# A graph layer on one core: features, destinations and penalties loaded two chunks at a time in three buffers, where four chunks at a time in two buffers were loaded before

## The chip, the core and the metric

The kernel runs on one core of one Trainium2 chip. The core has five instruction streams that wait for each other only through semaphores: PE (matrix multiply; loads of its stationary operand are shown apart as PEld), DVE (vector), ACT (scalar functions), POOL (GpSimd) and SP (SyncE, which here only issues transfers). ACT and SP issue plain transfers, GpSimd the indirect ones. The metric is the device time of one execution in microseconds; the median of the runs counts.

## The reference, cut to what matters

```python
h = maximum(layernorm(x), 0)                      # x: 12500 nodes x 32
e_feat = concatenate([h[src], h[dst], edge_attr]) # 400000 edges, sorted by dst
v = relu(e_feat @ W1 + b1) @ W2 + b2              # 96 -> 64 -> 32
x_cand = segment_max(v, dst, num_segments=12500)
return x + maximum(x_cand, h)
```

## The kernel before, in words

The edges are cut into four stripes of 100000, and a stripe into 196 chunks of C = 512 edges. One chunk of all four stripes is handled at once: partition = stripe x 32 features, 512 edges along the free axis. The first layer is a sum of three parts, each a product with a slice of W1, added up in four PSUM tiles `ph`: the edge's own features `ea` (L506), the destination's part, and the source's part `ht` (L548).

The **source** features come in two ways. For each chunk, 12 of 16 groups of 128 edges are fetched by GpSimd: one indirect transfer each (L154), from the normalised node table `h_d` in device memory into tiles `gh`, three to a tile, 24 tiles in turn; DVE then transposes each tile (L256). The other 4 groups are made by PE with one-hot matrices (`tile`, L238): 14 matmuls for each group of 128 edges, against the node features held on chip; DVE and ACT make the one-hots (L207, L216, L217), and DVE picks the right node of each result (L242, L243). Source indices of all chunks are on chip from the start.

The **destination** part uses that edges are sorted: a chunk's destinations lie in a window of 32 nodes. A window of precomputed products is fetched from `q_d` to `qw` (L456, four small transfers a chunk, their addresses read into SP's registers), and a one-hot `of` of destination against window row is made by ACT from `db`, the chunk's destinations repeated over 32 partitions (L462, L463).

After the second layer (L569), DVE's scan (L576) takes the running maximum along the edges; `pb`, a penalty of -1e30 at each first edge of a node, restarts it. Transposes and small matmuls (L476, L486) pick the last edge of each node, ACT copies them to `wo` (L490), and SP writes them to `top_d` (L494, four a chunk). Every write to one of the two `top_d` tables waits for the one before it there.

**Passes.** The loop of L530 handles two chunks in a pass, 98 passes in all. Its code is in a hand-written order, which is kept on SP, PE, DVE and ACT; GpSimd's stream is the gathers, in order. A pass for chunks c, c+1 does, in this order: GpSimd's gathers for c+2, c+3 (L533); the keys `kb` for the one-hots (ACT's queue, L192); `load` for chunks c+4, c+5 (L536); sometimes a block of destination data (`load_block`, L539, ACT's queue); then the matmuls, DVE and ACT work, among which `hid` (L552, needs `ph` complete), `window_hots` for the next pair (L554), `edges_into` and `windows_into` for the next pair (L564, L570), and `leave_1`, `leave_2`, which end the present one.

**`load`** (L437 to L457) is what the change touches. Where the chunk number divides by LOAD it issues three transfers: `ea` on SP, `db` and `pb` on ACT's queue (for the first chunks, before the loop, all on SP: L514). They serve LOAD chunks. With LOAD = 4 that is 1024 KB of `ea`, 1024 KB of `db`, 512 KB of `pb` in every second pass, into two buffers each. For each chunk it also issues the four `qw` transfers on SP, behind the `ea`. `load` runs AHEAD = 4 chunks before the chunk is used. SP's own order in a pass is thus: `ea`, eight `qw`, four `top_d` for chunk c-1, four for chunk c.

**Semaphores.** The framework gives all plain transfers of SP and ACT eight completion semaphores in turn, in one order for both queues, and GpSimd's gathers another eight. A transfer may be issued only when the earlier one that used its semaphore has landed; a queue waits for that, and what is behind waits too.

**Start and end.** Before the loop the nodes are normalised, `h_d` and `q_d` written, and the one-hot tiles of the first two chunks made. After it the two `top_d` tables are read back, their maximum is taken, and the output written (L620 to L703).

Of the kernel before, what the change touches and what calls it, by code (L numbers as in the profile page):

```python
# [8 lines left out]
F32 = mybir.dt.float32  # L9
F32R = mybir.dt.float32r  # L10
F16 = mybir.dt.float16
BF16 = mybir.dt.bfloat16
I32 = mybir.dt.int32
# [10 lines left out]
P = 128  # L24
# [8 lines left out]
C = 512  # L33
# [4 lines left out]
SE = E // NS  # L38
TS = S // P
EP = NS * S  # L40
LOAD = 4
A1 = 7
A0 = NT // A1
MM = 4
# [4 lines left out]
NB = NCH // BLOCK  # L49
# [11 lines left out]
def ap(t, offset, dims):  # L61
    return bass.AP(tensor=t.tensor, offset=t.offset + offset, ap=dims)
# [3 lines left out]
def gnn_kernel(ctx, tc, x, src, src_mm, src_t, dst, dst_ext, lo, lo_c, ends_b, edge_attr, weights, w1, w2, b2, out):  # L66
# [81 lines left out]
    def gather(c):  # L148
        n = min(K - MM * (c in MMC), (SE - c * C) // D)
        parts = []  # L150
        for k in range(0, n, SOME):
            parts.append(gathered.tile([P, SOME, D], F32, name="gh"))
            for i in range(min(SOME, n - k)):
                nc.gpsimd.indirect_dma_start(  # L154
                    out=parts[-1][:, i, :], out_offset=None, in_=h_d[:, :],
                    in_offset=bass.IndirectOffsetOnAxis(ap=src_i[:, c, k + i:k + i + 1], axis=0))
        return parts
# [14 lines left out]
    loaded_b, ats = {}, {}  # L172
# [14 lines left out]
    def load_keys(c, queue=nc.scalar):  # L187

        if c in MMC:
            n = min(2, MMC.stop - c)  # L190
            kb = early.tile([P, 2, MM * P], F16, name="kb", bufs=2)
            queue.dma_start(kb[:, :n], ap(key_d, (c - MMC.start) * MM * P,  # L192
                                           [[0, P], [MM * P, n], [1, MM * P]]))
            for k in range(n):
                keys[c + k] = kb[:, k]
# [31 lines left out]
    def tile(c, m):  # L227

        if c not in MMC:
            return  # L230
        if m == 0:
            mm_rows[c] = early.tile([P, MM, D], F32, name="gm", bufs=6)
        hot = hots[c]
        e = slice(m * P, (m + 1) * P)
        po = early_ps.tile([P, C], F32, name="pv", bufs=2)[:, :D * A0]
        for k in range(A1):
            for part in range(2):
                nc.tensor.matmul(po, hot[:, k, e], hs[:, part, k].rearrange("p f a -> p (f a)"),  # L238
                                 start=(k == 0 and part == 0), stop=(k == A1 - 1 and part == 1))
        of_group = po.rearrange("p (f a) -> p f a", a=A0)  # L240
        one = early.tile([P, D, A0], F32, name="one", bufs=2)
        nc.vector.tensor_tensor(one, of_group, masks[c][:, m, None, :].to_broadcast([P, D, A0]), op=ALU.mult)  # L242
        nc.vector.tensor_reduce(mm_rows[c][:, m, :], one, axis=AX.X, op=ALU.max)  # L243
# [21 lines left out]
    def load_block(b, queue=nc.scalar):  # L265
        edges = early.tile([P, 2, NS * BLOCK, J], I32, name="di")
        queue.dma_start(edges, dst[:, b])
        ends = early.tile([P, 2, NS * BLOCK], I32, name="ends")
        queue.dma_start(ends, ap(ends_b, b * 2 * NS * BLOCK, [[0, P], [NS * BLOCK, 2], [1, NS * BLOCK]]))
        loaded_b[b] = edges[:, 0], edges[:, 1], ends[:, 0], ends[:, 1]  # L270
# [160 lines left out]
    with tc.tile_pool(name="edges", bufs=3) as pool, tc.tile_pool(name="edges_ps", bufs=1, space=PSUM) as ps:  # L431
# [5 lines left out]
        def load(c, queue=nc.scalar):  # L437
            if c % LOAD == 0:
                n = min(LOAD, NCH - c) * C
                ea = pool.tile([P, LOAD * C], F32, name="ea", bufs=2)  # L440
                nc.sync.dma_start(ea[:, :n], ea_v[:, c * C:c * C + n])
                db = pool.tile([P, LOAD * C], I32, name="db", bufs=2)
                pb = pool.tile([P, LOAD * C], BF16, name="pb", bufs=2)
                queue.dma_start(db[:, :n], ap(dst_ext, 1 + c * C, [[S, NS], [0, D], [1, n]]))
                queue.dma_start(pb[:, :n], ap(pen_d, c * C, [[S, NS], [0, D], [1, n]]))
                for k in range(c, min(c + LOAD, NCH)):
                    loaded[k] = [t[:, (k - c) * C:(k - c + 1) * C] for t in (ea, db, pb)]
            if c % 2 == 0:
                _, base = nc.values_load_multi_w_load_instructions(
                    lo_i[0:1, c:c + 2], engines=[SP], min_val=0, max_val=N,  # L450
                    skip_runtime_bounds_check_because="dst is a node, or N where the host pads")
                for k in range(2):
                    bases[c + k] = base[k * NS:(k + 1) * NS]
            qw = pool.tile([P, HID], F32, name="qw", bufs=8)
            for s in range(NS):
                nc.sync.dma_start(qw[s * W:(s + 1) * W, :], q_d[bass.ds(bases[c][s], W), :])  # L456
            windows[c] = qw, bases.pop(c)  # L457

        def window_hots(c):

            of = ofs[c] = pool.tile([P, C], F32, name="of", bufs=3)
            nc.scalar.activation(of, loaded[c][1], AF.Square, bias=below[:, c:c + 1])  # L462
            nc.scalar.activation(of, of, AF.Relu, bias=ones, scale=-1.0)  # L463
# [66 lines left out]
        for c in range(0, NCH, 2):  # L530
            a, b = c + 2, c + 3
            for k in range(a, min(a + 2, NCH)):
                gh[k] = gather(k)  # L533
            load_keys(a + 2)
            for k in range(c + AHEAD, min(c + AHEAD + 2, NCH)):
                load(k)  # L536
            b_next = (c + 3 * AHEAD) // BLOCK
            if c % LOAD and b_next < NB and b_next not in ats and b_next not in loaded_b:
                load_block(b_next)  # L539

            if a == NCH - 2:
                nc.gpsimd.tensor_tensor(again.rearrange("p (g a) f -> p g a f", a=A0),
                                        hs[:, 0].rearrange("p g f a -> p g a f"),
                                        hs[:, 1].rearrange("p g f a -> p g a f"), op=ALU.add)
            tile(a, 0)
            to_features(a, 0)
            ht = [hts.pop(c + x).rearrange("p k e -> p (k e)") for x in range(2)]
            into_ph(ph, [(w1a, ht[x]) for x in range(2)], False, True)  # L548
            hid = []
            for s in range(NS):  # L550
                hid.append(pool.tile([P, C], F32, name="hid", bufs=6))
                nc.scalar.activation(hid[s], ph[s], AF.Relu, bias=b1c)  # L552
            for k in range(a, min(a + 2, NCH)):
                window_hots(k)  # L554
            one_hots_act(b)
            one_hots(b, 0, 2)
            tile(a, 1)
            to_features(a, 1)
            one_hots(b, 2, BY_ACT.start)
            mask_of(b)  # L560
            tile(a, 2)
            to_features(a, 2)
            last = [lasts(c)]
            ph = edges_into(a)  # L564
            pv = [early_ps.tile([P, C], F32, name="pv", bufs=2) for x in range(2)]
            for s in range(NS):
                for x in range(2):
                    g = slice(x * HID, (x + 1) * HID)
                    nc.tensor.matmul(pv[x][s * D:(s + 1) * D], w2x[g], hid[s][g], start=True, stop=True)  # L569
            windows_into(a, ph)  # L570
            leave()
            sms = []
            for x in range(2):
                before = -LOW if sm is None else sm[:, C - 1:C]
                sm = pool.tile([P, C], F32, name="sm", bufs=3)
                nc.vector.tensor_tensor_scan(sm, loaded.pop(c + x)[2], pv[x], before, op0=ALU.add, op1=ALU.max)  # L576
                sms.append(sm)
            tile(a, 3)
            one_hots_act(a + 2)
            to_features(a, 3)  # L580
            to_features(a, J)
            so = leave_1(c, sms[0])
            last.append(lasts(c + 1))
            tile(b, 0)
            to_features(b, 0)
            one_hots(a + 2, 0, 2)
            leave_2(c, so, last[0])
            tile(b, 1)
            to_features(b, 1)
            so = leave_1(c + 1, sms[1])  # L590
            one_hots(a + 2, 2, BY_ACT.start)
            mask_of(a + 2)
            tile(b, 2)
            to_features(b, 2)
            if c == 2 * AHEAD:
                places(FIRST, len(MMC))
            if (c + 4) % BLOCK == 0 and (c + 4) // BLOCK < NB:
                make_block((c + 4) // BLOCK)
            tile(b, 3)
            to_features(b, 3)  # L600
            to_features(b, J)
            leave = lambda c=c + 1, so=so, last=last[1]: leave_2(c, so, last)
# [164 lines left out]
```

## Time and profile before

| what | value |
|---|---|
| time, median of 3 runs | 4203.63 us (4203.39 to 4204.59) |
| the profiled execution's own time | 3066.27 us |
| its span, first to last instruction | 3064.5 us |
| mean granted clock of PE in it | 0.988 |
| PE busy | 2969.0 us, 97% of the span |
| GpSimd busy | 2261.8 us, 74% |
| DVE busy | 2246.8 us, 73% |
| ACT busy | 1089.8 us, 36% |
| transfers | 229.58 MB, 75 GB/s over the span |

The profiled execution is 1137 us shorter than the median of the runs. Durations below are of the profiled one.

The profile gives, for each engine, its busy time, and for groups of like instructions their number, busy time, mean duration in ns and the idle time of the engine just before them, with what ended most of it. "issue" there is time in which the engine waited for nothing that the profile shows. The waits name who waited for whom, with the total in us, how often, and the longest; the release is inferred from semaphores, so where a name had long been done, it was something else. All times within the run count from the start of the span. Since a plain matmul's end is modelled, a busy PE is not PE at its peak.

### The profile page before, as it was taken

Reading aid. Unit: us, or ns where it says so; the run is one execution under the profiler, and the core shown is the slowest. Engines: PE = TensorE matmul, PEld = TensorE weight load, DVE = VectorE, ACT = ScalarE, POOL = GpSimd, SP = SyncE. Lnnn points to the kernel's source line nnn. Section 1 sums busy time; section 2 is a strip of 40 time slices with the busy share of each in tenths; the row PEclk is TensorE's granted clock in tenths of the full one; section 3 lists DMA queues with packets and bytes.
Section 4 is the critical chain, followed back from the end, with each engine's and each line's share of the span. In section 5 each row is a group of like instructions: output and inputs, shape, how many; then the busy total and the mean of one; then the engine's idle time right before and its main releaser. Section 6 shows DMA issues by size and latency. Waiting matters only on the chain. (4 is left out here: it accounts for less than half of the span.)

```text
span 3064.5 us, 58825 instructions
## 1 busy us (share of the span) xinstructions
PE 2969.0 (97%) x21189; PEld 2326.1 (76%) x21189; DVE 2246.8 (73%) x3869; ACT 1089.8 (36%) x1795; POOL 2261.8 (74%) x2376
## 2 busy tenths in 40 slices
PE   5999999999999999999999999999999999999995
PEld 4678787787878777777777777777777777787773
DVE  6577777777777776777777777777777777777775
ACT  4333433333343333333333333333333333333331
POOL 6777777777777777777777777777777777777774
PEclk9899999999999999999999999999999999999997
DMA  7333333234324323332333233333332333333322
GB/s 245 70 85 66 62 79 82 60 66 84 71 59 88 74 59 66 81 76 59 65 82 73 59 69 80 70 63 65 86 70 59 73 82 65 63 70 81 66 57 70
DMA packets 194678, 229.58 MB, mean 75 GB/s; under 512 B 118333, under 2 KB 158797, under 8 KB 181582
## 3 DMA queue, kind: packets, MB, share of 16 engines
q10 hardware_dynamic: 32580, 110.55, 12.6%
q1 hardware_dynamic: 86762, 76.67, 10.8%
q0 software_dynamic: 75040, 38.57, 10.1%
q8 instruction: 167, 2.74, 0.4%
q14 instruction: 129, 1.06, 0.1%
HBM read 211.68 MB, written 13.85 MB: 74 GB/s over the span
## 5 line engine op out<-in xcount | busy, mean ns | idle before, releaser
L154 POOL DMA_INDIRECT gh<-h_d,src_i x2345 | 2241.7, 956 | 758.1 <-issue 537.4
L238 PE MATMUL pv<-hs,hot 128*128 128x448 f32 x10920 | 2359.8, 371 | 13.0 <-DVE sm L576 12.8
L238 PEld LDWEIGHTS pv<-hs,hot 128*128 128x128 f32 x10920 | 2016.0, 188 | 276.0 <-issue 71.0
L242 DVE TENSOR_TENSOR one<-pv,mask 128x448 f32<-128x448 f32 x780 | 483.5, 620 | 676.1 <-PE pv L238 674.6
L552 ACT ACTIVATE hid<-ph,wt 128x512 f32<-128x512 f32 x392 | 237.6, 689 | 1255.7 <-PE ph L500 1164.5
L207 DVE TENSOR_TENSOR hot<-kb,consts 128x1536 fp32r<-128x1536 f16 (+2 forms) x388 | 565.8, 1458 | 0.1
L243 DVE TENSOR_REDUCE gm<-one 128x32 f32<-128x448 f32 x780 | 483.7, 620 | 26.9
L217 ACT ACTIVATE hot<-away,ones 128x512 fp32r<-128x512 f32 x392 | 283.7, 724 | 251.4 <-issue 241.8
L216 ACT ACTIVATE away<-kb,key_n 128x512 f32<-128x512 f16 x392 | 278.0, 709 | 0.0
L256 DVE STREAM_TRANSPOSE ht<-gh 128x96 f32<-128x96 f32 x782 | 210.4, 269 | 68.8 <-DMA gh<-h_d,src_i 67.4
L576 DVE TENSOR_TENSOR_SCAN sm<-pb,sm,pv 128x512 f32<-128x512 bf16 x195 | 247.6, 1270 | 16.2 <-PE pv L569 5.9
L486 PEld LDWEIGHTS tr<-so,last 128*64 128x64 f32 x3136 | 108.4, 138 | 114.2 <-issue 78.7
L490 ACT ACTIVATE wo<-tr 128x64 f32<-128x64 f32 x196 | 44.0, 224 | 391.3 <-PE tr L486 374.0
L462 ACT ACTIVATE of<-db,below 128x512 f32<-128x512 int32 x196 | 141.7, 723 | 19.1 <-DMA db<-in_dst_ext 19.1
L569 PE MATMUL pv<-hid,wt 64*32 64x512 f32 x1568 | 135.1, 606 | 10.0 <-DVE one L242 8.9
L463 ACT ACTIVATE of<-of,ones 128x512 f32<-128x512 f32 x196 | 142.1, 725 | 6.4
L486 PE MATMUL tr<-so,last 128*64 128x64 f32 x3136 | 135.7, 229 | 3.7 <-DVE so L478 3.7
L500 PE MATMUL ph<-of,qw 32*64 32x512 f32 x1568 | 116.6, 623 | 15.6 <-DMA qw<-q_d 15.6
L468 DVE TENSOR_TENSOR last<-consts,at 128x512 f32<-128x512 f32 x196 | 129.9, 663 | 0.0
L478 DVE TENSOR_TENSOR so<-tr,wt 128x512 f32<-128x512 f32 x196 | 127.8, 652 | 2.3 <-PE tr L476 2.3
L476 PE MATMUL tr<-ident,sm 128*128 128x128 f32 x784 | 118.1, 273 | 1.1 <-ACT wo L490 1.1
L500 PE MATMUL ph<-ht,wt 32*64 32x512 f32 x1568 | 114.0, 617 | 0.0
(77 smaller groups left out, 554.4 us busy)
## 6 DMA issues: line engine op xcount, KB each, us to landing
ea<-in_edge_attr SPq DMA_DIRECT2D x49, 1024.0 KB
db<-in_dst_ext ACTq DMA_DIRECT2D x48, 1024.0 KB
gh<-h_d,src_i POOLq DMA_INDIRECT x2345
pb<-pen_d ACTq DMA_DIRECT2D x48, 512.0 KB
kb<-key_d ACTq DMA_DIRECT2D x95, 256.0 KB
qw<-q_d SPq DMA_DIRECT2D x784, 8.0 KB
top_d<-wo SPq DMA_DIRECT2D x784, 4.0 KB
top_d<-zero ACTq DMA_DIRECT2D x2, 1568.0 KB
```

Of the source, the lines that this page charges most:

```text
L154: nc.gpsimd.indirect_dma_start(out=parts[-1][:, i, :], out_offset=None, in_=h_d[:, :], in_offset=bass.IndirectOffsetOnAxis(ap=src_i[:, c, ...
L207: nc.vector.tensor_tensor(hot_of(c)[:, start:stop], keys[c][:, None, :].to_broadcast([P, n, MM * P]), key_ps[:, start:stop, None].to_broad ...
L216: nc.scalar.activation(away, keys[c], AF.Square, bias=key_n[:, k:k + 1])
L217: nc.scalar.activation(hot_of(c)[:, k], away, AF.Relu, bias=ones, scale=-1.0)
L238: nc.tensor.matmul(po, hot[:, k, e], hs[:, part, k].rearrange("p f a -> p (f a)"), start=(k == 0 and part == 0), stop=(k == A1 - 1 and par ...
L242: nc.vector.tensor_tensor(one, of_group, masks[c][:, m, None, :].to_broadcast([P, D, A0]), op=ALU.mult)
L243: nc.vector.tensor_reduce(mm_rows[c][:, m, :], one, axis=AX.X, op=ALU.max)
L256: nc.vector.transpose(ht[:, r].rearrange("p k e -> p (k e)"), gh[c][part][:, :r.stop - r.start].rearrange("p k f -> p (k f)"))
L486: nc.tensor.matmul(pw[g * 2 * W:(g + 1) * 2 * W], last[:, j, 2 * g:2 * g + 2].rearrange("p s w -> p (s w)"), so[:, j, g * 2 * D:(g + 1) * ...
L500: nc.tensor.matmul(ph[s][x * HID:(x + 1) * HID], w[g], e[g], start=start, stop=stop)
L552: nc.scalar.activation(hid[s], ph[s], AF.Relu, bias=b1c)
L576: nc.vector.tensor_tensor_scan(sm, loaded.pop(c + x)[2], pv[x], before, op0=ALU.add, op1=ALU.max)
```

## The change

LOAD becomes 2. The three tiles of `load` lose their own `bufs=2` and take the pool's three buffers. The condition for `load_block` named LOAD and now names the number 4, so blocks are loaded in the same passes as before. Each set of transfers is half as large, and a set is issued in every pass. The buffers of the three tiles shrink from 2 x 20 KB to 3 x 10 KB in each partition. PE's, DVE's and GpSimd's instructions, and their order, are the same in both built programs.

```diff
-LOAD = 4
+LOAD = 2
...
         def load(c, queue=nc.scalar):
             if c % LOAD == 0:
                 n = min(LOAD, NCH - c) * C
-                ea = pool.tile([P, LOAD * C], F32, name="ea", bufs=2)
+                ea = pool.tile([P, LOAD * C], F32, name="ea")
                 nc.sync.dma_start(ea[:, :n], ea_v[:, c * C:c * C + n])
-                db = pool.tile([P, LOAD * C], I32, name="db", bufs=2)
-                pb = pool.tile([P, LOAD * C], BF16, name="pb", bufs=2)
+                db = pool.tile([P, LOAD * C], I32, name="db")
+                pb = pool.tile([P, LOAD * C], BF16, name="pb")
                 queue.dma_start(db[:, :n], ap(dst_ext, 1 + c * C, [[S, NS], [0, D], [1, n]]))
                 queue.dma_start(pb[:, :n], ap(pen_d, c * C, [[S, NS], [0, D], [1, n]]))
...
             b_next = (c + 3 * AHEAD) // BLOCK
-            if c % LOAD and b_next < NB and b_next not in ats and b_next not in loaded_b:
+            if c % 4 and b_next < NB and b_next not in ats and b_next not in loaded_b:
                 load_block(b_next)
```

## What was predicted

> **What bounds the kernel now.** I read the page's engine rows first, then its costliest groups, then GpSimd's timeline in one loop pass, then the stretches of three passes, then the waits (engines, then the queue of SyncE).
>
> ```profile
> PE 2969.0 (97%) x21189; PEld 2326.1 (76%) x21189; DVE 2246.8 (73%) x3869; ACT 1089.8 (36%) x1795; POOL 2261.8 (74%) x2376
> L154 POOL DMA_INDIRECT gh<-h_d,src_i x2345 | 2241.7, 956 | 758.1 <-issue 537.4
> ```
>
> PE at 97% looks like the bound, but GpSimd's 74% misleads: its idle time is mostly the pause after each gather. Three rows of its timeline:
>
> ```profile
> 1543.97 0.96 POOL L154 DMA_INDIRECT gh<-h_d,src_i  x1 [0.30 <-DMA gh<-h_d,src_i]
> 1545.23 0.95 POOL L154 DMA_INDIRECT gh<-h_d,src_i  x1 [0.30 <-issue]
> 1547.20 0.95 POOL L154 DMA_INDIRECT gh<-h_d,src_i  x1 [1.01 <-DVE gm L243]
> ```
>
> One gather starts every 1.26 us at best (0.95 and 0.30). A pass needs 24, so 30.24 us of GpSimd; a pass in which PE never waits lasts 29.73 us (the stretch 1507.42 to 1537.15, one start of the L500 `ht` matmuls to the next). So GpSimd is slower by 0.5 us a pass and lives on its lead: gathers start at 27.7, the loop's first `ht` matmuls at 88.9. By about 1190 the lead is used up, and from there every second pass is longer:
>
> ```profile
> 1507.42:1537.15 29.73, 29.73 (x217) 23.56 (x216) 24.11 (x45) 10.90 (x18) 22.72 (x24) 1.00 0.29 50
> 1537.15:1568.50 31.35, 30.92 (x217) 23.78 (x216) 22.44 (x39) 10.89 (x18) 23.14 (x25) 1.00 0.39 87
> ```
>
> (stretch, its length, busy PE, PEld, DVE, ACT, POOL, granted clock, DMA share, GB/s.) The long pass is the one after a load was issued (L444 at 1525.6, L441 at 1534.5). Its waits are small and one-directional: a gather is late, DVE's transpose L256 waits for it, PE's L569 waits for DVE:
>
> ```profile
> DVE ht L256 <- DMA gh<-h_d,src_i: 61.6, 73, 2.4
> PEld pv L569 <- DVE one L242: 53.5, 60, 2.3
> ```
>
> (waits from 1190 to 3014.) PE's passes from there exceed 29.73 by about 50 us in all. The end, then, follows GpSimd's stream: last gather at 3014.0, then 50.5 us of tail. The stream has 758.1 us of idle; 12.6 is the wait for the first `h_d`, 2344 pauses of 0.305 are 714.9, and 30.6 us remain as real stalls. Sorting those by time since the last L444 issue gives the place: all but 1 us of them lie 12 to 28 us after it, 63 gathers with a pause over 0.4 us, at 48 loads.
>
> Why there: the gathers have eight completion semaphores in turn, so a gather may not start before the one eight earlier has landed, 8 x 1.26 = 10.1 us later. From the trace's semaphore records I took each gather's time to its last increment: 2.4 us (median) 34 to 58 us after a load, but 8.5 to 9.7 us in the first 14 us after it, with a ninth decile of 10.2 to 10.4. The burst puts gathers just over that limit. From 24 to 26 us, when `pb` with its 4096-byte packets is what is left, it is 5.0.
>
> **The change, part by part.** [...]`ea`, `db`, `pb` become 98 transfers each instead of 49, half as large, one set each pass.
>
> Issues. 48 more `db` and 48 more `pb` on ACT cost 0.56 and 0.51 us: 51 us, behind ACT's wait for PE ahead of L552 (1164.5 us in 91 passes, 12.8 each); without that cover `hid` would be 51 us late. 49 more `ea` on SyncE cost 0.42: 21 us, hidden since SyncE sits 15 us late in load passes today and PE does not notice. On GpSimd nothing.
>
> Waits. SyncE's `qw` transfers share eight semaphores with ACT's loads, and today the queue stands behind them:
>
> ```profile
> SPq L456 <- DMA db<-in_dst_ext: 612.6, 49, 14.4
> SPq L456 <- DMA pb<-pen_d: 180.3, 48, 5.3
> ```
>
> That is 16 us a load. The built program keeps such waits, now in every pass: the fourth `qw` on `db`, the sixth on `pb`, the eighth on `ea`. ACT issues `db` about 9 us ahead of SyncE's `ea`, and half of 14.4 is 7.2, so `db` lands before SyncE asks; I take 0 to 4 us for `pb` and `ea`. Behind them stand the `qw` rest and eight `top_d` writes; both have most of a pass to spare, so 0. ACT's `db`, `pb` wait for semaphores last used by the previous `qw` and by the first four `top_d`, all issued by then: 0 to 1 us, under the 12.8. [...]A third buffer frees before it is asked for: its last reader, the scan, ended six us before the next issue (1519.4 against 1525.6).
>
> Gathers, the main term. Half-size transfers have packets of 4096 bytes (`pb` 2048) where 8192 took 586 and 402 ns (queues q1, q10) and 4096 took 159. The nearest row for a 4096-byte burst is the 5.0 us above; add 1 to 2 us for `ea` beside it: 6 to 7 us, well under 10.1. So stalls go from 30.6 to about 0 (value taken: 0.6 left). The bounds: all 30.6 gone, or none, and below nothing the second rival.
>
> The Trainium skill speaks against this: "DMA: Bandwidth & Descriptors", section "Bandwidth", says to batch transfers to 1 MiB or more, with a fixed cost near 2 us each. By it 147 more transfers cost 294 us of transfer time, some of it exposed. By the rows, `db` of 1 MB takes 14 us, 75 GB/s, so size isn't its limit, and the queues fill 33.5% of the engines (12.6, 10.8, 10.1); the fixed cost lies under a pass. I take the rows. The same page, "Queues, rings and completion order", says each engine alternates between the queues by whole packets. By it a gather's packet waits for one packet of each other queue, 586 + 402 ns, so 2.4 becomes 3.4 us, the limit of 10.1 is never met, and the change gains 0 (4203). The rows say 8.7, so more than one packet stands ahead; I keep the rows, and take only that a smaller packet shortens the wait.
>
> Start. PE stands for the first loads: ACT waits 19.1 us for the first `db`, PE 10.5 and 2.5 us for `qw` (77.7, 81.5; SyncE held by `db`, then `pb`), and the granted clock is 0.5 from 72 to 89 us. Half a `db` lands about 10 us earlier, at 62; `pb` at 66; the last needed `qw` at 69. So `windows_into` ends at about 70 instead of 83.4, 13 us, and some of the half clock goes too. But chunks 2 and 3 now come in a second set, whose `qw` wait for `db` and `pb` of two sets together: PE may wait 5 us at 84, where today it waits 4.3. Net 8 to 18 us for PE, and in this profile worth 0: GpSimd started at 27.7 regardless, and PE merely meets it sooner.
>
> Sum on the profiled execution: 3066.3 (span 3064.5, 1.8 around it) - 30 = 3036. PE alone would allow about 3064.5 - 50 - 13 = 3001, so GpSimd is next late, at 30.2 a pass. The medians need a caution: the runs shown take 4203.6, 1137 us above the profiled one, and nothing in the trace says which resource is slower there. Carried over as an absolute amount, 4203.6 - 30 = 4174; in proportion it would be -41, 4162.
>
> **The rivals.**
> - *The gather stalls go, the stream sets the end (likeliest, 0.48):* 4174, down to 4155 if the slower runs have longer bursts.
> - *Only the start counts (0.22):* if PE is what is slower in the runs shown (a pass of about 41 us), gathers are never late and no stall is exposed. For it: PE's clock is the one resource that varies in the trace (1.0, halves at start and end). Gain 4 to 15 us: 4192, about half of it beyond 0.2%.
> - *Nothing moves (0.14):* if gathers are slower there, 1.7 us each, then eight of them last 14 us, over the 9.7 of the burst, and there is no stall to remove: 4203. That the stated halving has no effect on the end is this case too.
> - *Slower (0.16):* bursts come in 97 passes instead of 48, and `ea`, issued 9 us after `db`, joins the gathers' wait. If latency in a burst stays above 10.1 us, each costs what one costs now, 30.6 / 48 = 0.64 us: 97 x 0.64 = 62, so +31: 4235. It decides if halved packets leave more than 10.1 us; against it is the 5.0 row.
>
> **How the numbers follow.** About 0.2% (8 us) is what a measurement of this kernel can tell from no change. Faster: 0.48 + half of 0.22 + a little = 0.61; same: the other half and most of 0.14, 0.23; slower 0.16. Range 4150 to 4212: from the proportional gain with 12 us more to just past no change; it leaves out most of the slower case and a larger gain, under 0.2.
>
> **What would show it.** GpSimd's L154 row: idle 758 falls to about 730, few pauses over 0.4 us; gather landing in a burst 6 to 7 us; passes alternate no more, all about 30.2; last gather near 2984. SyncE's wait on `db` falls from 612 to under 100. First `ht` matmuls near 75. Wrong if pauses stay or come in every pass, if the wait of ACT ahead of L552 vanishes, or if the profile gains its 30 us and the median does not: then what is slower in the unprofiled runs hides the stream.

## The result, and the profile after

The changed kernel took 4283.69 us (median of 5 runs, 4272.22 to 4292.48), the kernel before beside it 4204.29 us (4203.39 to 4208.16): a ratio of 1.0185, 95% interval 1.0171 to 1.0199. It is slower by 79 us, where 30 us of gain were predicted.

One thing has to be said first, since no number below can be read without it: **both kernels have two conditions, the same for all timed runs of one set, and the kernel before takes about 3060 us in one and about 4200 us in the other.** It is not the chip: one chip took 4199 us for the kernel before in one set and 3066 us in a later one. The times above and the profile after are of the second; the profiled execution of the kernel before, from which every duration of the prediction came, was of the first (3066.27 us). I call them the 3060 and the 4200 condition after the time of the kernel before. In the 3060 condition the changed kernel is **faster**: 3026.48 us (4 runs) against 3063.16, ratio 0.9875 (0.9849 to 0.9902).

The profile after is an execution of 4277.61 us, span 4275.5. From its page, the engines, the granted clock in 40 slices, the gathers, and the one-hot matmuls with the idle time before them:

```profile
PE 3533.0 (83%) x21189; PEld 2435.1 (57%) x21189; DVE 2238.1 (52%) x3869; ACT 1111.9 (26%) x1795; POOL 2263.7 (53%) x2376
PEclk7789899999898989899898889898989998988898
L154 POOL DMA_INDIRECT gh<-h_d,src_i x2345 | 2243.1, 957 | 1893.5 <-DVE ht L256 703.5
L238 PE MATMUL pv<-hs,hot 128*128 128x448 f32 x10920 | 2614.8, 385 | 605.1 <-issue 417.6
```

The number of instructions is that of before, and a gather takes 957 ns, as before (956). But GpSimd now waits 1893.5 us, the largest part of it (703.5) for DVE instead of in its own pauses: it is early, not late. DVE's transposes, which need the gathered rows, no longer wait for them; here is their row, first of the kernel before at 3060 (e1_before_again, below), then of the profile after:

```profile
L256 DVE STREAM_TRANSPOSE ht<-gh 128x96 f32<-128x96 f32 x782 | 210.5, 269 | 67.4 <-DMA gh<-h_d,src_i 67.0
L256 DVE STREAM_TRANSPOSE ht<-gh 128x96 f32<-128x96 f32 x782 | 209.8, 268 | 0.0
```

And PE has idle time, 605.1 us ahead of the one-hot matmuls alone, most of it put down to "issue": PE waits for nothing that the profile shows.

The stretches of one pass in the middle and of two near the end (stretch, its length, busy PE, PEld, DVE, ACT, POOL with the number of instructions, granted clock, DMA share, GB/s):

```profile
1869.38:1912.86 43.48, 36.03 (x217) 25.48 (x217) 22.78 (x42) 11.10 (x18) 22.92 (x25) 0.88 0.22 49
4155.25:4184.99 29.74, 29.74 (x217) 23.57 (x216) 22.19 (x38) 10.90 (x18) 11.95 (x1) 1.00 0.20 55
4184.99:4214.72 29.73, 29.73 (x217) 23.56 (x216) 22.19 (x38) 10.89 (x18) 0.00 (x0) 1.00 0.03 7
```

The 216 matmuls of a pass (the view counts one more, cut by the edge) take 43.48 us in the middle and 29.73 at the end. So the condition isn't a slower PE for the whole run. It goes with the gathers, whose last one starts at 4150.8, and not with the loads: the pass from 4155.25 still has a whole set of them (`db` issued at 4173.4, `ea` at 4179.3; 55 GB/s). Inside the slow pass, PE's weight loads show what it is (start, length, group with its count, idle time before and what ended it):

```profile
1870.42 4.18 PEld L238 LDWEIGHTS pv<-hs,hot 128*128 128x128 f32 x21 [0.81 <-issue]
1875.78 0.30 PEld L238 LDWEIGHTS pv<-hs,hot 128*128 128x128 f32 x2 [1.17 <-issue]
1877.92 0.28 PEld L238 LDWEIGHTS pv<-hs,hot 128*128 128x128 f32 x1 [1.84 <-issue]
1878.63 0.29 PEld L238 LDWEIGHTS pv<-hs,hot 128*128 128x128 f32 x1 [0.43 <-issue]
1880.03 0.28 PEld L238 LDWEIGHTS pv<-hs,hot 128*128 128x128 f32 x1 [1.11 <-issue]
```

Up to 1874.4 a weight load starts every 0.20 us. Then they come at distances of 0.7 us and its multiples (1877.92, 1878.63, 1880.03), until about 20 us into the pass. SyncE's register instructions do the same: 293 of them take over 0.3 us, nearly all about 0.7, where none does in the 3060 condition. DVE, ACT and GpSimd keep their durations. I call this the **slow stretch**; every pass of the 4200 condition has one, in the kernel before too. The weight loads shown wait for no semaphore, so their idle time stands as "issue"; waits whose release the profile can't name stand as "remote". The granted clock follows it: 0.84 in the 3 us from 1875.38, then 0.50 in the 3 us from 1878.38. (That a PE with little to do loses half its clock is what the Trainium skill says too, "TensorE: Matmul & The Clock Gate", Part 1; here the half clock lasts about 8 us in each pass, 974 us in all, against 58 in the 3060 condition.)

### The profile page after: what moved, and what is told of

Same layout as the page of the kernel before. It is cut to its first block, busy times and chain, and to the rows that moved or that the text cites. A ratio compares the mean times of both kernels' runs of the same rounds, so it can differ in the third digit from the quotient of the medians.

```text
span 4275.5 us, 59032 instructions
## 1 busy us (share of the span) xinstructions
PE 3533.0 (83%) x21189; PEld 2435.1 (57%) x21189; DVE 2238.1 (52%) x3869; ACT 1111.9 (26%) x1795; POOL 2263.7 (53%) x2376
## 2 busy tenths in 40 slices
DMA packets 214672, 229.60 MB, mean 54 GB/s; under 512 B 119510, under 2 KB 159974, under 8 KB 214119
## 5 line engine op out<-in xcount | busy, mean ns | idle before, releaser
L154 POOL DMA_INDIRECT gh<-h_d,src_i x2345 | 2243.1, 957 | 1893.5 <-DVE ht L256 703.5
L238 PE MATMUL pv<-hs,hot 128*128 128x448 f32 x10920 | 2614.8, 385 | 605.1 <-issue 417.6
L238 PEld LDWEIGHTS pv<-hs,hot 128*128 128x128 f32 x10920 | 2058.2, 194 | 1061.6 <-issue 622.0
L552 ACT ACTIVATE hid<-ph,wt 128x512 f32<-128x512 f32 x392 | 260.6, 687 | 2211.7 <-remote 1016.9
L569 PE MATMUL pv<-hid,wt 64*32 64x512 f32 x1568 | 251.3, 903 | 8.7 <-DVE one L242 7.9
L486 PEld LDWEIGHTS tr<-so,last 128*64 128x64 f32 x3136 | 124.6, 146 | 199.4 <-issue 169.0
L500 PE MATMUL ph<-ea,wt 32*64 32x512 f32 x1568 | 225.4, 1016 | 13.2 <-issue 13.0
L486 PE MATMUL tr<-so,last 128*64 128x64 f32 x3136 | 162.7, 239 | 51.9 <-issue 47.8
L569 PEld LDWEIGHTS pv<-hid,wt 64*32 64x32 f32 x1568 | 37.2, 128 | 230.2 <-issue 118.8
L500 PE MATMUL ph<-of,qw 32*64 32x512 f32 x1568 | 150.4, 825 | 0.1
L500 PE MATMUL ph<-ht,wt 32*64 32x512 f32 x1568 | 127.1, 622 | 7.8 <-issue 5.1
```

The source lines that it names most:

```text
L154: nc.gpsimd.indirect_dma_start(out=parts[-1][:, i, :], out_offset=None, in_=h_d[:, :], in_offset=bass.IndirectOffsetOnAxis(ap=src_i[:, c, ...
L486: nc.tensor.matmul(pw[g * 2 * W:(g + 1) * 2 * W], last[:, j, 2 * g:2 * g + 2].rearrange("p s w -> p (s w)"), so[:, j, g * 2 * D:(g + 1) * ...
L500: nc.tensor.matmul(ph[s][x * HID:(x + 1) * HID], w[g], e[g], start=start, stop=stop)
```

## The experiments

All of them are compared with the kernel before, run beside them. The first set, the third and the last two fell in the 3060 condition, the second in the 4200 condition; a set's condition can't be chosen.

**What the stalls are worth at 3060.** First the kernel before again (e1_before_again), 3062.83 us.

> The kernel before, unchanged, to see its trace at its usual time of 4204 us (the profile shown before was of a run of 3066 us). In the changed kernel's trace nearly every pass has one slow stretch of about 8 us in which SyncE's and PE's instructions take 0.7 us each, and the granted clock drops after it; the last two passes, which load nothing, have none and last 29.7 us. Theory S, a stretch comes with each set of loads: here passes alternate, about 30 us without a load and 53 us with one. Theory T, a stretch comes in every pass whatever is loaded: all passes about 41 us. Theory G, the one of the prediction (late gathers in the bursts): passes of 41 us in which GpSimd never waits for DVE.

It repeats the profile of the prediction: 31.4 us of gather pauses beyond 0.305, 63 of them over 0.4 us, first `ht` matmuls at 85.3, clock 0.988, and two passes of

```profile
1323.12:1352.98 29.86, 29.86 (x218) 23.70 (x217) 22.26 (x39) 10.89 (x18) 22.65 (x24) 1.00 0.30 56
1352.98:1384.14 31.16, 30.58 (x217) 23.66 (x216) 22.37 (x38) 10.89 (x18) 23.41 (x26) 1.00 0.38 92
```

Then smaller transfers without a change of pass: LOAD stays 4, but each transfer is issued as two halves, one behind the other, in the same pass, so that packets are half as large and transfers twice as many.

```diff
-                ea = pool.tile([P, LOAD * C], F32, name="ea", bufs=2)
-                nc.sync.dma_start(ea[:, :n], ea_v[:, c * C:c * C + n])
+                ea = pool.tile([P, LOAD * C], F32, name="ea", bufs=2)
+                for h in range(0, n, 2 * C):
+                    nc.sync.dma_start(ea[:, h:h + 2 * C], ea_v[:, c * C + h:c * C + h + 2 * C])
...
```

> Four chunks every second pass in two buffers as before, but each transfer of ea, db and pb issued as two halves: packet sizes and counts of the changed kernel, with the timing of the kernel before. If the smaller packets or their number are what costs, about 4284 us (1.018 to 1.02 of before); if it is that a load comes in every pass, 4204 us (within 0.3%). The prediction's theory G would have it faster by up to 30 us.

Measured 3026.78 us, ratio 0.9899 (0.9879 to 0.9920) to a kernel before of 3057.04; pauses 31.4 to 1.0. As many bytes in the same pass, in packets of half the size, give nearly the whole gain.

Next, each half of the change alone: only `ea`, then only `db` and `pb`, by two chunks in three buffers.

```diff
-LOAD = 4
+EA = 2
+DB = 4
...
-                ea = pool.tile([P, LOAD * C], F32, name="ea", bufs=2)
+                ea = pool.tile([P, EA * C], F32, name="ea", bufs=2 if EA == 4 else 3)
...
```

> Only ea, on SyncE's queue, two chunks at a time in three buffers; db and pb four chunks in two buffers as before. If SyncE's queue in each pass is the cause (ea ahead of the eight qw), 4270 to 4290 us; if it is db and pb on ACT's queue, 4204 us.

> Only db and pb, on ACT's queue, two chunks at a time in three buffers; ea four chunks in two buffers. The mirror of the run with only ea: 4270 to 4290 us if the loads on ACT's queue (and SyncE's waits for them) are the cause, 4204 us if it is ea. If both parts cost, each gives some 4240 us.

Measured 3035.37 (0.9930, 0.9909 to 0.9951) and 3024.97 (0.9892, 0.9872 to 0.9913). The gathers' rows of the pages, first of e1_before_again, then e3_only_ea, then e4_only_db_pb (busy, mean ns, idle before):

```profile
L154 POOL DMA_INDIRECT gh<-h_d,src_i x2345 | 2236.8, 954 | 758.3 <-issue 538.1
```
```profile
L155 POOL DMA_INDIRECT gh<-h_d,src_i x2345 | 2236.1, 954 | 734.1 <-issue 548.3
```
```profile
L155 POOL DMA_INDIRECT gh<-h_d,src_i x2345 | 2236.0, 954 | 726.6 <-issue 551.4
```

Idle time falls by 24 us for one and by 32 for the other. Each removes most of the stalls, and the gains don't add (the whole change gains 36.7, in a later set, and `db` and `pb` alone 37.0 there): once a gather lands within the 10.1 us, landing sooner is worth nothing. A gather issued 4 to 14 us after a load lands in 8.8 to 9.6 us (medians of 2-us steps) in e1, 7.2 to 8.4 in e3, and 6.0 falling to 3.2 in e4.

**The changed kernel again, and further down, at 4200.** This set fell in the 4200 condition: kernel before 4199.24 us (7 runs). The changed kernel, LOAD = 1 with six buffers, and the kernel before once more:

```diff
-LOAD = 4
+LOAD = 1
...
-                ea = pool.tile([P, LOAD * C], F32, name="ea", bufs=2)
+                ea = pool.tile([P, LOAD * C], F32, name="ea", bufs=6)
...
```

> The changed kernel, unchanged, beside runs of the kernel before on the same chip. In the call before this one the kernel before took 3057 us and none of its passes had the slow stretches of the changed kernel's trace. Theory G (late gathers in the bursts): where the kernel before takes about 3057 us, this takes 3020 to 3035 us (0.988 to 0.993), GpSimd's stalls 31 us become under 2; where it takes about 4204 us, no gain. Theory S (each set of loads brings a slow stretch): about 1.02 of before on any chip, 3110 us beside 3057.

> LOAD = 1 with six buffers: ea, db and pb four times as many as before and a quarter as large (2048 and 1024 bytes a packet). Theory G: no stalls of gathers, as with two chunks, 3020 to 3035 us beside a kernel before of 3057. Where the slow stretches are there (before 4204 us): if the number of packets or issues lengthens them, the step from four chunks to two (+80 us) goes on, to 4340 to 4450 us; if not, 4284 us or less.

> The kernel before, unchanged, once more for its trace. If this chip runs it in about 4204 us: theory S, passes alternate between 30 and 53 us; theory T, every pass about 41 us with one slow stretch each, some shorter than the changed kernel's. If it runs in about 3057 us, the same trace as last time: passes of 29.7 us, from some 1200 us on every second of them 1 to 2 us longer.

Measured 4262.57 (1.0154, 1.0133 to 1.0176), 4292.36 (1.0216, 1.0187 to 1.0245) and 4202.66. The loss repeats and grows with the number of load sets, though less than in proportion: half a set a pass 4199, one set 4263, two sets 4292, which is neither of the two figures expected for it. Either each load brings a stretch (S), or every pass has one whatever it loads (T). The passes of the kernel before, which loads in every second one, hardly alternate here (41.88 and 41.40 us on the average), so S is out.

Where in a pass the time goes I read by counting matmuls: the mean time from one to a later one over some 80 passes, worked out from the traces, in us (number in the pass; the first `ht` matmul is 0).

| stretch of the pass | 3060, changed (e9) | 4200, before (e8) | 4200, changed | changed - before |
|---|---|---|---|---|
| 0 to 35: `ht`, first one-hots | 5.25 | 5.23 | 5.28 | +0.05 |
| 35 to 60: one-hots, `ea` | 2.97 | 8.03 | 9.06 | +1.03 |
| 60 to 92: `hid`, `qw` | 2.14 | 5.71 | 4.16 | -1.55 |
| 92 to 108: `last` (L486) | 0.62 | 0.87 | 1.64 | +0.77 |
| 108 to 122: one-hots | 2.96 | 3.69 | 4.02 | +0.33 |
| 122 to 176: one-hots | 7.82 | 7.82 | 7.82 | 0.00 |
| 176 to 216: one-hots | 8.27 | 10.30 | 10.35 | +0.05 |

The slow stretch lies between the 35th and the 122nd matmul (about 10 us lost), with a smaller one after the 176th (2 us). In the changed kernel it begins earlier, 5.2 us after the first `ht` matmul instead of about 7, and lasts further into L486. The sum of the last column is +0.68 a pass: over the whole run the changed profile has 73.8 us more from its first `ht` to its last than e8 (97 passes, 0.76 each) of 74.7 in the span; its first `ht` is at 170.4 against 169.6, its tail the same.

One instruction stream does change near that place. In the kernel before at 4200, SyncE runs next to nothing in the first 9 us of a pass: behind a load it stands at a `qw` transfer that waits for `db` and goes on about 11 us into the pass; in the other passes it has issued its `qw` about 3 us ahead of the pass and then waits for ACT's `wo` until 22 us into it. With the small `db` it goes on sooner. Its waits, of e8_before_again and of the profile after (at 4200 these sums are too small, since most semaphore increments are missing from the record, see below):

```profile
SPq L456 <- DMA db<-in_dst_ext: 260.2, 21, 14.1
SPq L456 <- DMA pb<-pen_d: 75.8, 24, 4.3
```
```profile
SPq L456 <- DMA db<-in_dst_ext: 64.6, 49, 3.4
SPq L456 <- DMA pb<-pen_d: 48.1, 16, 3.7
```

So between 0 and 9 us after the first `ht`, SyncE runs 0.02 instructions a pass in e8, 10.5 in the profile after and 10.6 in e5; its register instructions over 0.3 us rise from 198 to 293. Two theories follow. O: SyncE's window instructions, now just ahead of the slow stretch and at its start, take turns with PE there. P: it is the number of transfers and packets in all (194679 before, 214672 after, 254658 with LOAD = 1).

**Telling O from P, and the changed kernel at 3060.** The changed kernel and the three partial ones stand side by side here, so that they split the loss, or the gain, in whichever condition they meet.

> The changed kernel itself, unchanged. If the kernel before takes about 3057 us here, theory A (the gathers' stalls of 31 us go, nothing else is lost) expects 3020 to 3032, ratio 0.988 to 0.992, with GpSimd's excess gaps under 5 us; the rival (two-chunk loads cost something of their own in every pass, about 0.7 us) expects 3090 or more. If the kernel before takes about 4200 us, both expect 4260 to 4285, ratio 1.014 to 1.020, as twice before.

> Packets of two chunks, but both halves issued in the same pass and buffers of four chunks. If the kernel before takes about 4200 us: theory P (more and smaller packets cost the slow stretches) expects the whole loss, 4255 to 4285; theory O (it is that SyncE and ScalarE have loads to issue in every pass, so that SyncE is still at the windows' instructions when the slow stretch comes) expects under half of it, 4200 to 4230. If before takes about 3057: 3027 as measured before, ratio 0.988 to 0.992.

> Only the features by two chunks in three buffers; SyncE issues this load. If before takes about 4200 us: theory O (SyncE's order) expects nearly the whole loss, 4245 to 4285, theory P (packets: 1/3 of the added ones) 4215 to 4230. If before takes about 3057: 3035, ratio 0.991 to 0.995.

> Only dst and the penalties by two chunks in three buffers; ScalarE issues these. If before takes about 4200 us: theory O (SyncE's order) expects 4195 to 4215, theory P (2/3 of the added packets) 4240 to 4260. If before takes about 3057: 3025, ratio 0.987 to 0.991.

It was 3060 (kernel before 3063.16, 7 runs). Changed kernel 3026.48 (0.9875, 0.9849 to 0.9902), halves 3028.60 (0.9884, 0.9858 to 0.9910), only `ea` 3037.88 (0.9910, 0.9883 to 0.9937), only `db` and `pb` 3026.19 (0.9877, 0.9851 to 0.9903). The numbers for 3060 hold for all four, and O and P stay untold. The changed kernel's page, two passes, and SyncE's waits:

```profile
L154 POOL DMA_INDIRECT gh<-h_d,src_i x2345 | 2235.3, 953 | 727.6 <-issue 545.9
L238 PE MATMUL pv<-hs,hot 128*128 128x448 f32 x10920 | 2357.3, 371 | 0.0
```
```profile
1273.40:1303.67 30.27, 30.27 (x217) 23.74 (x216) 24.12 (x45) 10.88 (x18) 22.94 (x25) 1.00 0.32 70
1303.67:1334.05 30.38, 30.38 (x217) 23.76 (x217) 22.88 (x41) 10.89 (x18) 23.07 (x25) 1.00 0.32 69
```
```profile
SPq L456 <- DMA pb<-pen_d: 304.4, 97, 4.2
SPq L456 <- DMA db<-in_dst_ext: 150.4, 82, 5.8
```

No pauses are left (one over 0.4 us, against 63), and long passes no longer alternate with short ones. From 1190 us on the passes last 30.15 us on the average (29.7 to 31.5), against 30.48 in e1_before_again; that is GpSimd's pace, 24 gathers of 1.257 us.

Then, for O, both kernels without the `qw` loads after chunk 4 (the first four windows are used again), and for what feeds the stretch both without gathers after chunk 8 (gathered rows of earlier chunks are used again). These leave part of the computation out.

```diff
-            qw = pool.tile([P, HID], F32, name="qw", bufs=8)
-            for s in range(NS):
-                nc.sync.dma_start(qw[s * W:(s + 1) * W, :], q_d[bass.ds(bases[c][s], W), :])
-            windows[c] = qw, bases.pop(c)
+            if c < AHEAD:
+                qws[c] = pool.tile([P, HID], F32, name="qw", bufs=8)
+                for s in range(NS):
+                    nc.sync.dma_start(qws[c][s * W:(s + 1) * W, :], q_d[bass.ds(bases[c][s], W), :])
+            windows[c] = qws[c % AHEAD], bases.pop(c)
```
```diff
+        if 8 <= c and n == K - MM:
+            return gh_first[c % 4]
-        parts = []
+        parts = gh_first[c % 4] = []
```

> The kernel before, with the gathers left out from chunk 8 on (the gathered rows of the first chunks are used again; the rest of the work stays). If the kernel before takes about 3060 us here: theory A (the time saved is the time in which gathers come late) expects 2995 to 3020, and the same time as the changed kernel without gathers within 5 us; the rival (the smaller loads save time of their own) expects it 20 us or more above that one. If before takes about 4200: if the gathers feed the slow stretches, the passes fall to about 30 us and the time to 3000 to 3200; if PE and SyncE make them by themselves, it stays above 3900.

> The changed kernel, with the gathers left out from chunk 8 on in the same way. If before takes about 3060: theory A 2995 to 3020, within 5 us of the kernel before without gathers. If before takes about 4200: as for the kernel before without gathers; if the loss of 60 to 80 us lies in the loads and SyncE's order, it stays; if it needs the gathers, it goes to under 20 us.

> The kernel before, with the qw loads left out from chunk 4 on (the first four windows are used again), so that SyncE has only the features and the top_d stores to issue. If before takes about 3060: the gathers still come late in the burst, 3035 to 3062. If before takes about 4200: theory O (SyncE's instructions share the slow stretch with PE) expects 3900 to 4150, theory P (packets and records in all) 4150 to 4200.

> The changed kernel, with the qw loads left out from chunk 4 on. If before takes about 3060: 25 to 35 us under the kernel before without them, as with them. If before takes about 4200: theory O expects it within 25 us of the kernel before without them, since SyncE has nothing left to issue at the start of the slow stretch; theory P expects 50 to 90 us above it, as with them.

3060 again (kernel before 3065.64, 15 runs). Without gathers 3016.77 (0.9844, 0.9827 to 0.9860) and 3003.08 (0.9802, 0.9785 to 0.9818). My "within 5 us" was wrong: they differ by 13.7. But their passes are alike, 29.75 and 29.76 us, and the difference is the start: first `ht` at 86.0 and 70.4. With the gathers gone PE sets the end, and then the earlier start counts in full; with them it counts for next to nothing (e10 starts at 88.5 and takes 3028.60, e9 at 70.6 and takes 3026.48). Two passes of f1_before_no_gathers, with POOL empty:

```profile
1286.93:1316.66 29.73, 29.73 (x217) 23.57 (x217) 24.12 (x45) 10.89 (x18) 0.00 (x0) 1.00 0.32 79
1316.66:1346.52 29.86, 29.86 (x218) 23.65 (x217) 22.25 (x39) 10.88 (x18) 0.00 (x0) 1.00 0.20 46
```

The burst is still there (79 GB/s), and no pass is longer for it: loads cost PE nothing, they cost only by way of late gathers. Without windows 3061.33 (0.9985, 0.9975 to 0.9996) and 3024.63 (0.9871, 0.9855 to 0.9888): they are 36.7 us apart, as with the windows, so the window loads take no part at 3060.

Three of these were run once more, for the other condition.

> Again the kernel before without the qw loads from chunk 4 on, for a chip where the kernel before takes about 4200 us. There theory O (SyncE's window instructions share the slow stretch with PE) expects 3900 to 4150, theory P (packets and records in all) 4150 to 4200. Where before takes about 3060: 3050 to 3070, as measured.

> Again the changed kernel without the qw loads from chunk 4 on. Where before takes about 4200: theory O expects it within 25 us of the kernel before without them, theory P 50 to 90 us above it. Where before takes about 3060: 3020 to 3030, as measured.

> Again the kernel before without the gathers from chunk 8 on. Where before takes about 4200: if the gathers feed the slow stretches, passes of about 30 us and 3000 to 3200; if PE and SyncE make them by themselves, above 3900. Where before takes about 3060: 3010 to 3022, as measured.

3060 once more (kernel before 3068.51): 3065.33 (0.9990, 0.9982 to 0.9999), 3028.96 (0.9874, 0.9857 to 0.9890) and 3015.35 (0.9831, 0.9814 to 0.9847). O and P are thus **not told apart** by these runs; no run without windows or without gathers met the 4200 condition.

The traces at 4200 go further, because their passes differ among themselves.

- *The stretch comes with gathers alone.* Every second pass of e8 has no `ea`, `db`, `pb` or `qw` in flight and no SyncE instruction in its first 16 us, only the packets of gathers (294 on the average). From the 35th to the 92nd matmul these passes take 13.72 us. The passes behind a load have 605 packets of loads and windows in the same 16 us, and SyncE runs 15 instructions between those matmuls; they take 13.71 us (42 passes of each kind; 5.11 in e9). So inside the stretch neither SyncE's turns nor the loads' packets cost PE anything that can be seen.
- *It doesn't come with loads alone.* The first pass without gathers, 4155.25 to 4184.99 in the profile after, has 508 packets of loads and windows in its first 16 us, twice as many as the passes in the middle (244), and lasts 29.74 us; the next one has SyncE's last windows in its first 3.7 us and lasts 29.73. In e5, e6 and e8 too the passes without gathers last 29.7 us.

So the stretch itself needs the gathers, or something that goes with them. What makes it longer by 0.7 us a pass in the changed kernel, these readings don't tell: only that the window instructions come earlier, ahead of it, is left of O, and that is untested.

## Why the prediction was wrong

**The step that failed is the carry-over:** "Carried over as an absolute amount, 4203.6 - 30 = 4174". The sum of 30 us was made on an execution whose end follows GpSimd, and laid on runs whose end follows PE. A pass of e8_before_again in the middle, and its gathers:

```profile
1877.16:1918.75 41.59, 36.76 (x218) 25.03 (x217) 23.54 (x42) 11.21 (x18) 23.07 (x25) 0.92 0.25 46
L154 POOL DMA_INDIRECT gh<-h_d,src_i x2345 | 2241.9, 956 | 1819.9 <-DVE ht L256 689.0
```

At 4200 a pass takes 41.6 us, GpSimd needs 30.24 and is idle for 1819.9 us, the largest part (689.0) waiting for DVE. The last `ht` comes 81.6 us after the last gather, against 8.0 at 3060. Gathers that land late in the burst delay nobody there, so the term is 0, not -30. The prediction named its own doubt, that nothing in the trace said which resource was slower there. A gap of 1137 us between profile and median was the largest number on the table, and it deserved more than a caution: that the engine which the gain needs as the bound was the bound in those runs too was never shown.

**The second step is what the change costs PE, put at nothing:** "hidden since SyncE sits 15 us late in load passes today and PE does not notice", and "0" for the waits. At 3060 that holds. At 4200 PE's slow stretches cost 0.76 us more in each of 97 passes, 74 us; with the 30 us that could not be gained, that makes 104 of the 110 us missed. Shown is where the loss lies, that it repeats (4283.69 and 4262.57 in two sets), and that the stretch goes with the gathers. **Why the changed kernel lengthens it stays open**, and so does what the stretch is: only PE and SyncE slow down, in steps of about 0.7 us, and the DMA packets themselves are not slower (a 1024-byte row of a gather takes 119 ns in e8, 115 in e1).

The recording is a suspect. Semaphore increments are missing from it at 4200 all through a pass, also in its first 4 us, where PE runs at full rate: e8 has 30722 on record where the same program has 73548 in e1, 301 a pass against 738. From the first pass without gathers on, which is also the first without a stretch, next to nothing is missing any more (483 in e8, 493 in the same pass of f1). But every run here was recorded, so none shows the kernel without it. The Trainium skill, "NOTIFIC — the notification-queue block", section 7.1, says that the path of such records can hold an engine up; no run here shows that it does.

**Point by point, at 3060, where the durations came from:**

- *GpSimd's stream bounds the kernel:* right. Without gathers the time falls by 49 us, and passes are 29.75.
- *Gathers land late in the burst, and half-size packets bring 6 to 7 us:* right. Medians 8.4 to 9.6 us before, 4.7 to 6.5 after, in the first 12 us after a load. Pauses 31.4 to 0 (0.6 left was predicted); passes 30.15 on the average from 1190 us on, though single ones still differ by up to 1.7 us (all about 30.2 was predicted); idle of L154 727.6 (about 730), last gather at 2977.2 (near 2984).
- *Sum 3036:* 3026.48 (and 3001 for PE alone: 3003.08 without gathers). Of 36.7 us, 31.4 are the pauses; the last gather starts 32.9 us earlier, and the last `ht` follows it after 3.8 us instead of 8.0.
- *Issues and waits cost 0:* right for the sum. SyncE's wait on `db` fell to 150.4, not under 100, and that on `pb` rose to 304.4 from 178.4, 3.1 a set, within the 0 to 4 taken.
- *Start 8 to 18 us earlier, worth 0:* right, 85.3 to 70.6, worth about 2 here and 13.7 once gathers are gone.
- *"Bandwidth" on the Trainium skill's page "DMA: Bandwidth & Descriptors":* transfers of 1 MB cut in half make the kernel 1% faster. The rule is about bandwidth, and at 75 GB/s that is not what limits here. The 2 us stand in another section of that page, "Anatomy of one DMA — SWDGE (gpsimd) path", as a fit for transfers that GpSimd issues; SyncE and ScalarE issue these.
- *"Queues, rings and completion order" there:* the prediction took one row of 8192 bytes for the packet that an engine finishes before it turns to another queue, and got 3.4 us. The page's packet is "≈9-17 descriptors typical". A 1 MB transfer has 128 rows, 8 for each of 16 engines; if 8 rows of `ea` and 8 of `db` stand ahead, the estimate by that rule is 2.4 + 8 x (0.586 + 0.402) = 10.3 us, and 5.0 with the 4096-byte rows of e9 (0.169 and 0.159). Measured were 8.4 to 9.6 and 4.7 to 6.5. So the rule isn't refuted here; its packet was misread.

**The rivals.** "Only the start counts" had the right premise, passes of about 41 us and gathers never late, but the start doesn't move there: first `ht` at 169.6 and 170.4. "Slower" had the right sign by the wrong mechanism: it laid the loss on gathers in more bursts, at 4235, and the gathers are early.

## What to carry to other kernels

Smaller transfers can be the faster ones where something short and urgent shares the DMA engines with them, and the test is the landing time of the urgent ones against the time that their semaphores or buffers allow, not the bandwidth. Before a sum made on one execution is laid on other runs, see that the same engine bounds both: with a third more time in the runs, a gain found in a stream that has only 0.5 us a pass to lose is most likely covered. And read the ends of a trace: there the passes lose one kind of work after another, and that tells what a slow stretch needs.

## What the hardware showed that I had not expected

- The same program in two conditions, 3060 and 4200 us, each steady within a set to 0.5% (15 runs: 3062.58 to 3075.41; 7 runs: 4195.33 to 4206.73), with PE and SyncE at one instruction per 0.7 us for part of every pass in the slower one.
- In that condition the granted clock halves in each pass for about 8 us, 933 us in all against 74, though the passes at its very end run at 1.00.
- There, PE's slow stretch comes in passes with only gathers in flight and is gone in passes with only loads (29.74 us against 42 to 44).
- Halving packets from 8192 to 4096 bytes, with the same bytes in the same pass, took a gather's landing from 8.8 to 9.6 us down to 7.1 to 7.2 (e1 and e2, 4 to 8 us after a load) and removed 30 us of stalls.
